# Graph attention, last stage: the low parts are made from a copy of the high parts in PSUM

## The chip, the cores and the metric

The kernel runs on one core of a Trainium2 chip. The metric is the device time of one execution in microseconds (us). Given for the kernel before are the times of three executions, and one more execution that the hardware profiler recorded.

The engines go by their names in the profile: PE (TensorE, matrix products; PEld is its weight load), DVE (VectorE), ACT (ScalarE), POOL (GpSimd, which here also issues the indirect DMAs that gather rows) and SP (SyncE, which issues the other DMAs).

## The reference

Two layers of a relational graph attention network over 3125 nodes of 768 numbers and 53125 edges that are sorted by their target node; then the input is added and each row is normalised. For each layer:

```python
xr = jnp.einsum('nd,rdf->rnf', x, W)          # three relations
oi = xr[etype, dst]
oj = xr[etype, src]
alpha = jax.nn.leaky_relu(oi @ q + oj @ k, 0.2)
m = jax.ops.segment_max(alpha, dst, num_segments=n_nodes)
e = jnp.exp(alpha - m[dst])
z = jax.ops.segment_sum(e, dst, num_segments=n_nodes)
a = e / (z[dst] + EPS)
msg = (a[:, :, None] * oj.reshape(-1, heads, out_ch)).reshape(-1, heads * out_ch)
out = jax.ops.segment_sum(msg, dst, num_segments=n_nodes) + b
```

The first layer has four heads of 192, the second one head of 768. Between them stands an elu; at the end `_layernorm(x + out)`. Everything is float32.

## The kernel before

The kernel has four parts in a row: the sorting data of the edges and the attention weights (`prepare`, `weights_kq`, `nodes_kq`), the first layer's rows and attention (`phase1`), the first layer's sums over edges together with the second layer's rows (`phase2`), and the last stage, `phase3`: the second layer's attention, its sums over edges, the residual and the normalisation. A second kernel stands behind an `If` for edge lists that do not fit the layout; it does not run with these inputs. The change is in `phase3` alone.

**Tiling.** The targets are cut into 25 blocks of 128 nodes (NB). A block's edges are cut into slots of 128 edges: 18 slots for each block (SL), 9 for the last, 441 slots in all (NK). For a slot, POOL gathers 128 rows of 772 float32 numbers from the table `tab2` in HBM with one indirect DMA (`gather`, which calls `gather_rows`, line L451). A row holds the 768 features, the key's part of the attention score, a 1 for the sum of the weights, and padding. The rows land in `gs`, six tiles of six slots each, so 36 slots are held.

**Sums.** For each slot the kernel multiplies a 128x128 selection matrix (which edge goes to which node of the block) by the slot's 128x772 rows, weighted by `p`, the exponential of the attention score. The product is added up in PSUM over the slots of a block (`acc`, two banks, two buffers). There are two ways for it, and `whole(k)` says which one a slot takes:

- A whole slot is one product in float32. DVE makes `selp`, the selection with the weights in it (L1062), and PE multiplies it by the gathered rows G (L1091, the rows `acc<-G,selp`; four records each slot).
- A split slot is two products in the float32r type. ACT makes the high part `H = p * G`, rounded to float32r (L1066); DVE, or POOL for the last 18 slots, makes the selection `sel` of ones and zeros (L1071 or L1069); DVE makes the low part `L = p * G - H` (L1080, function `low`); PE multiplies `sel` by H and by L (L1091, rows `acc<-H,sel` and `acc<-L,sel`).

With `WHOLE = (13, 25)`, 13 of each 25 slots are whole; of the last 18 slots (`late`) each third is.

`selp` and `sel` compare a row of the numbers 0 to 127 with each edge's node. The row lies in SBUF as `row` (frow in the profile); `phase3` copies it into a PSUM bank of its own, `rowp` (L959), for VectorE.

**Attention of a block.** DVE spreads the edges' node numbers from a PSUM product `bc` into `sT` (L980 on PE, L986 on DVE, five times each block); PE looks up the query's part with it (`pq`, L1000), DVE reduces it (L1006, L1008), `a_alpha` adds the key's part out of the gathered rows (L1015, which needs the block's last gather) and makes the leaky relu (L1017); PE turns the scores (L1022), DVE finds each node's largest with two scans (L1028, L1030), ACT takes the exponential (`e`, L1037), PE turns it back (L1041), DVE copies it to `p` (L1046).

**End of a block.** `e_y` divides and adds the residual on DVE (L1102), `e_n` makes the statistics (L1109 to L1113), `e_sd` takes a square root on ACT (L1117), `e_low` follows on DVE (L1122, L1124), `e_out` scales on ACT (L1130) and SP stores the rows. ACT changes its function table twice a block, once for the exponential and once for the root.

**Order.** All engines run instructions in the order of one Python loop that is written out by hand, and wait for each other by semaphores. An iteration k does, in this order: the gather of slot k; the sums of slot k - LAG (LAG = 29); the events of k, which are the attention and end steps, set by `when(...)`; and then

```python
            if 0 <= k - LAG + 2 < NK:
                low(k - LAG + 2)
            if 0 <= k - LAG + 3 < NK:
                high(k - LAG + 3)
```

`high` makes `selp`, or H and `sel`. A block's steps come at fixed iterations: counted from the block's end e, alpha at e + 2, the turn at e + 3, the scans at e + 4, exp at e + 5, the turn back at e + 6 and `p` at e + 7. The block's end steps follow at e + 30 to e + 37.

**PSUM in this stage.** Eight banks: `acc` four, `bc`, `pq`, `pa` and `rowp` one each.

Of the kernel before, what the change touches and what calls it, by code (L numbers as in the profile page):

```python
# [8 lines left out]
F32 = mybir.dt.float32  # L9
F32R = mybir.dt.float32r  # L10
F16 = mybir.dt.float16
BF = mybir.dt.bfloat16
I32 = mybir.dt.int32
AF = mybir.ActivationFunctionType
ALU = mybir.AluOpType
# [5 lines left out]
P = 128  # L21
# [17 lines left out]
CAP = SL * P  # L39
# [5 lines left out]

PART = 6

WHOLE = (13, 25)


@with_exitstack
def kernel(
# [32 lines left out]
    RW = D + 4  # L85
    HW = RW // 2
    CW = F1 + 1
    LL = FRONT + E + BACK
    NK = (NB - 1) * SL + SLL
    V, S, G, T = nc.vector, nc.scalar, nc.gpsimd, nc.tensor  # L90
# [16 lines left out]
    row = keep.tile([P, P], F32, name="frow")  # L107
# [10 lines left out]
    dl = keep.tile([P, NB, SL], F32, name="fdl")  # L118
# [146 lines left out]
    def split_parts(work, pts, w, name="t"):  # L265

        parts = []
        for i, pt in enumerate(pts):
            H, L = (work.tile([P, 2, w if name != "t" else 2 * P], F32R, name=f"{name}{s}{i}",
                              bufs=2 if name == "t" else 1) for s in "HL")  # L270
            S.copy(H[:, :, :w], pt[:, :, :w])
            V.tensor_sub(L[:, :, :w], pt[:, :, :w], H[:, :, :w].bitcast(F32))
            parts.append((H, L))
        return parts
# [179 lines left out]
    def start(b, into):  # L454
        if b not in into:
            into[b] = nc.sync.value_load(starts[0:1, b:b + 1], min_val=0, max_val=E)
        return into[b]

    def at(t, rw, off, ap, s):

        c = t[rw:rw + 1, bass.ds(s + (FRONT + off), 1)]
        return bass.AP(tensor=c.tensor, offset=c.offset, ap=ap)
# [282 lines left out]
    def phase2(work, psum, wH, wL):  # L745
# [25 lines left out]
        def whole(k):  # L771

            return k < 8 and k % 2 == 1

        def high(k):
            b, j = slot(k)
            g = gs[k % NG]
            if whole(k):
                sel = work.tile([P, H1, P], F32, name="L", bufs=3)
                for h in range(H1):  # L780
# [12 lines left out]
        def low(k):  # L793
# [4 lines left out]
            H = st[k][1]  # L798
            L = work.tile([P, RW], F32R, name="L", bufs=3)
            for h in range(H1):  # L800
                c = slice(h * CW, (h + 1) * CW)
                V.scalar_tensor_tensor(L[:, c], g[:, c], pall[:, b, j, h:h + 1], H[:, c].bitcast(F32),  # L802
                                       op0=ALU.mult, op1=ALU.subtract)
# [139 lines left out]
    def phase3(work, psum):  # L943
# [8 lines left out]
            V.memset(t, 0.0)  # L952
        blk = {}
        st = {}
        one = work.tile([1, P], BF, name="one", bufs=1)
        V.memset(one, 1.0)

        rowp = psum.tile([P, 512], F32, name="rowp", bufs=1)[:, :P]
        V.tensor_copy(rowp, row)  # L959

        def gather(k):
            b, j = divmod(k, SL)
            gather_rows(gs[k // PART % NT][:, k % PART, :], tab2, b, j)

        def a_load(b):
            s = blk[b] = {}
            r0 = start(b, regs)
            s["f"] = work.tile([SL, 3 * P + 1], F32, name="f", bufs=2)
            nc.sync.dma_start(s["f"], at(ed_d, 3, -P - 1, [[P, SL], [1, 3 * P + 1]], r0))
            s["d"] = work.tile([1, CAP], BF, name="d", bufs=2)  # L970
            nc.sync.dma_start(s["d"], at(dr_d, 0, 0, [[CAP, 1], [1, CAP]], r0))

        def a_spread(b, i):
# [21 lines left out]
        def a_q2(b):  # L995
            s = blk[b]
            nq = R * 3
            pq = s["pq"] = psum.tile([P, 512], F32, name="pq", bufs=1)
            for j in range(SL):
                T.matmul(pq[:, j * nq:(j + 1) * nq], s["sT"][:, j * P:(j + 1) * P],  # L1000
                         q2s[:, b].rearrange("p r s -> p (r s)"), start=True, stop=True)
# [46 lines left out]
        def whole(k):  # L1048

            return k % 3 == 0 if late(k) else k * WHOLE[0] % WHOLE[1] < WHOLE[0]  # L1050

        def late(k):

            return k >= NK - SL

        def high(k):
            b, j = divmod(k, SL)
            g = gs[k // PART % NT][:, k % PART, :]
            p = blk[b]["p"][:, j:j + 1]
            if whole(k):  # L1060
                sel = work.tile([P, P], F32, name="selp", bufs=4)
                V.tensor_scalar(sel, rowp, dl[:, b, j:j + 1], p, op0=ALU.is_equal, op1=ALU.mult)  # L1062
                st[k] = [sel, g]
                return
            H = work.tile([P, RW], F32R, name="H", bufs=4)
            S.activation(H, g, AF.Copy, scale=p)  # L1066
            sel = work.tile([P, P], F32R, name="sel", bufs=4)
            if late(k):
                G.tensor_scalar(sel, row, dl[:, b, j:j + 1], None, op0=ALU.is_equal)  # L1069
            else:  # L1070
                V.tensor_scalar(sel, rowp, dl[:, b, j:j + 1], None, op0=ALU.is_equal)  # L1071
            st[k] = [sel, H]

        def low(k):
            if whole(k):
                return
            b, j = divmod(k, SL)
            g = gs[k // PART % NT][:, k % PART, :]
            L = work.tile([P, RW], F32R, name="L", bufs=3)
            V.scalar_tensor_tensor(L, g, blk[b]["p"][:, j:j + 1], st[k][1].bitcast(F32), op0=ALU.mult, op1=ALU.subtract)  # L1080
            st[k].append(L)

        def sums(k):
            b, j = divmod(k, SL)
            sel, *parts = st.pop(k)
            if j == 0:
                blk[b]["acc"] = psum.tile([P, 2, 512], F32, name="acc", bufs=2)
            acc = blk[b]["acc"]
            for i, a in enumerate(parts):
                for c in range(2):  # L1090
                    T.matmul(acc[:, c, :HW], sel, a[:, c * HW:(c + 1) * HW], start=(j == 0 and i == 0),  # L1091
                             stop=(k in ends and i == len(parts) - 1))
# [45 lines left out]
        LAG = SL + 11  # L1138
        for b in range(NB):
            when(max(b * SL - 12, 0), a_load, b)  # L1140
            for i in range(5):
                when(max(b * SL - 4, 2) + 2 * i, a_spread, b, i)
                when(max(b * SL - 4, 2) + 1 + 2 * i, a_spread2, b, i)
            for d, f in ((10, a_q), (11, a_q2), (12, a_q3)):
                when(max(b * SL - 4, 2) + d, f, b)
            e = min((b + 1) * SL, NK)
            for d, f in ((2, a_alpha), (3, a_turn), (4, a_scan), (5, a_exp), (6, a_back), (7, a_put)):
                when(e + d, f, b)
            if b + len(xbs) < NB:
                when(e + LAG + 20, x_load3, b + len(xbs))  # L1150
            for d, f in ((1, e_y), (2, e_n), (5, e_sd), (6, e_low), (8, e_out)):
                when(e + LAG + d, f, b)
        for k in range(max(ev) + 1):
            if k < NK:
                gather(k)
            if 0 <= k - LAG < NK:
                sums(k - LAG)
            for f, a in ev.get(k, []):
                f(*a)
            if 0 <= k - LAG + 2 < NK:  # L1160
                low(k - LAG + 2)
            if 0 <= k - LAG + 3 < NK:
                high(k - LAG + 3)

    with tc.manual_schedule():
        with tc.tile_pool(name="share", bufs=1) as pool:
# [4 lines left out]
            with tc.tile_pool(name="wbuf", bufs=1) as wbuf:  # L1171
                wH = wbuf.tile([P, R * DT, D + 2], F32R, name="wH")
                wL = wbuf.tile([P, R * DT, D + 2], F32R, name="wL")
                with tc.tile_pool(name="pre", bufs=1) as pre:
                    qq = pre.tile([P, NB, H1, R], F32, name="qq")
                    with tc.tile_pool(name="work0", bufs=1) as work, tc.tile_pool(
                        name="psum0", bufs=1, space=PSUM
# [21 lines left out]
                    with tc.tile_pool(name="work1", bufs=1) as work, tc.tile_pool(  # L1199
                        name="psum1", bufs=1, space=PSUM  # L1200
# [4 lines left out]
            with tc.tile_pool(name="work3", bufs=1) as work, tc.tile_pool(name="psum3", bufs=1, space=PSUM) as psum:  # L1205
                phase3(work, psum)
# [538 lines left out]
```

## Time and profile before

| | |
|---|---|
| three executions, median (lowest to highest) | 2476.31 us (2463.49 to 2496.46) |
| the profiled execution's own time | 2296.29 us |
| its span, first to last instruction | 2294.5 us |
| mean granted clock of PE in it | 0.955 |
| PE, PEld busy | 2047.2 us (89%), 1758.8 us (77%) |
| DVE busy | 1685.4 us (73%) |
| ACT busy | 1172.9 us (51%) |
| POOL busy | 1749.5 us (76%) |
| HBM read, written | 428.40 MB, 94.04 MB |
| PE, DVE, ACT, POOL busy in 1610 to 2247 us, of 637.00 | 548.84, 523.56, 262.61, 502.22 us |

Shares of busy time are means over stages that differ; what sets the time of a stage is read from a window of the trace that holds this stage alone. A line of a group gives the line of the kernel, the engine, the operation, the names of what it writes and reads, the shapes and the count; behind the bar the busy time in us and the mean duration in ns; behind the second bar how long the engine was idle just before these instructions, and what ended most of that ("issue" is idle time for which the profile shows no reason). A line of waits gives who waited for whom, the sum in us, how often, and the longest. A line of the timeline gives the start and the duration in us, and in brackets the idle time before it. Matmuls overlap in the records, so a busy PE is not a PE at its peak.

### The profile page before, as it was taken

What the parts mean: (1) busy time and instruction counts of PE and PEld (TensorE: products, weight loads), DVE (VectorE), ACT (ScalarE), POOL (GpSimd) and SP (SyncE); (2) the same over time, 40 slices, a digit from 0 to 9 for tenths busy, and PEclk for the clock granted to TensorE, in tenths of its full rate; (3) what the DMA queues carried; (4) which work ended last, traced back from release to release, by engine and by line L of the source; (5) the groups of instructions that cost most, each with busy time, mean ns of one, the idle gap of its engine ahead of it and who ended that gap; (6) DMA issues with size and microseconds to landing.
All of it is one profiled execution on the core that took longest, in us unless ns stands there. A gap on an engine that the chain in (4) does not pass through costs nothing.

```text
span 2294.5 us, 37251 instructions
## 1 busy us (share of the span) xinstructions
PE 2047.2 (89%) x11055; PEld 1758.8 (77%) x11055; DVE 1685.4 (73%) x4377; ACT 1172.9 (51%) x2620; POOL 1749.5 (76%) x1685
## 2 busy tenths in 40 slices
PE   6998878998885899999999999999498898899886
PEld 5888878888885889999999999999255555555554
DVE  7734434434432899999999999995388888898887
ACT  5411111111111788888888888884144444444443
POOL 4267777777776888888888888883777777777773
PEclk9999999999998899999999999999699999999998
DMA  6554544444455977778777777775888888888882
GB/s 178 179 154 158 177 137 158 165 153 143 158 191 166 316 237 232 228 231 244 236 229 234 230 234 238 232 231 202 282 280 293 288 296 279 286 278 283 282 269 72
DMA packets 153593, 508.20 MB, mean 221 GB/s; under 512 B 40404, under 2 KB 53723, under 8 KB 153383
## 3 DMA queue, kind: packets, MB, share of 16 engines
q0 software_dynamic: 85472, 334.19, 48.1%
q1 hardware_dynamic: 57681, 155.56, 18.8%
q10 hardware_dynamic: 10230, 15.98, 2.2%
q8 instruction: 91, 1.49, 0.3%
q14 instruction: 119, 0.97, 0.1%
HBM read 428.40 MB, written 94.04 MB: 228 GB/s over the span
## 4 chain that ended last, share of the span: by engine, by line
PE 35%; DVE 14%; POOL 7%; issue 6%; DMA 5%; ACT 1%; POOLq 0%; DVEq 0%; ACTq 0%
PE po L876 15%; PE acc L821 11%; PE acc L1091 7%; DMA G<-ftab,ridx 4%; DVE L L1080 4%; POOL share L451 3%; POOL sel L790 2%; DVE selp L1062 1%; DVE L L802 1%; DVE sT L986 1%; POOL G L451 1%; DVE sel L1071 1%; DMA G<-ftab,rfirst 1%; PE pt L851 1%; DVE stats L1109 1%
## 5 line engine op out<-in xcount | busy, mean ns | idle before, releaser
L788 ACT ACTIVATE H<-share,pall 128x193 fp32r<-128x193 f32 x1748 | 644.0, 447 | 106.9 <-DMA share<-ftab,ridx 43.5
L802 DVE SCALAR_TENSOR_TENSOR L<-share,pall,H 128x193 fp32r<-128x193 f32 x1748 | 648.9, 437 | 28.6 <-ACT H L788 14.1
L876 PE MATMUL po<-wH,hT 128*128 128x386 f32 (+1 forms) x1800 | 533.2, 339 | 0.0
L451 POOL DMA_INDIRECT G<-ftab,ridx x378 | 432.5, 1144 | 115.2 <-issue 54.0
L451 POOL DMA_INDIRECT kt<-kt,ridx x378 | 405.7, 1073 | 115.2 <-issue 114.6
L451 POOL DMA_INDIRECT share<-ftab,ridx x378 | 428.6, 1134 | 81.4 <-DVE L L802 42.6
L629 PE MATMUL po<-wH,xT 128*128 128x384 f32 x1584 | 445.2, 354 | 0.4 <-issue 0.2
L1091 PE MATMUL acc<-G,selp 128*128 128x386 f32 x904 | 355.5, 519 | 1.1 <-DVE selp L1062 1.1
L876 PEld LDWEIGHTS po<-wH,hT 128*128 128x128 f32 x1800 | 334.6, 189 | 0.6 <-DVE hT L864 0.5
L876 PE MATMUL po<-wL,hT 128*128 128x386 f32 (+1 forms) x900 | 304.9, 339 | 0.0
L629 PEld LDWEIGHTS po<-wH,xT 128*128 128x128 f32 x1584 | 302.1, 196 | 2.9 <-DVE xT L616 0.5
L629 PE MATMUL po<-wL,xT 128*128 128x384 f32 x792 | 275.4, 348 | 0.0
L821 PE MATMUL acc<-H,sel 128*128 128x386 f32 x874 | 241.9, 358 | 22.0 <-POOL sel L790 12.1
L641 ACT COPY share<-po 128x384 f32<-128x384 f32 x144 | 69.0, 479 | 339.4 <-PE po L629 274.4
L1091 PEld LDWEIGHTS acc<-G,selp 128*128 128x128 f32 x904 | 169.7, 199 | 89.1 <-issue 23.0
L790 POOL TENSOR_SCALAR sel<-frow,fdl 128x128 fp32r<-128x128 f32 x291 | 224.8, 773 | 13.4 <-PE acc L821 1.5
L821 PE MATMUL acc<-L,sel 128*128 128x386 f32 x874 | 226.5, 340 | 0.0
L1080 DVE SCALAR_TENSOR_TENSOR L<-G,p,H 128x772 fp32r<-128x772 f32 x215 | 217.5, 1013 | 1.4 <-issue 0.7
L1066 ACT ACTIVATE H<-G,p 128x772 fp32r<-128x772 f32 x215 | 189.8, 927 | 47.5 <-issue 34.0
L821 PEld LDWEIGHTS acc<-H,sel 128*128 128x128 f32 x874 | 149.8, 189 | 55.7 <-POOL sel L790 46.7
L565 DVE TENSOR_TENSOR a<-qe,kt 128x72 f32<-128x72 f32 x25 | 5.9, 238 | 242.3 <-DMA kt<-kt,ridx 205.3
L876 PEld LDWEIGHTS po<-wL,hT 128*128 128x128 f32 x900 | 169.7, 189 | 0.0
(229 smaller groups left out, 2902.8 us busy)
## 6 DMA issues: line engine op xcount, KB each, us to landing
ftab<-r SPq DMA_DIRECT2D x75, 386.0 KB
ftab<-share SPq DMA_DIRECT2D x72, 386.0 KB
sT<-dr_d SPq DMA_DIRECT2D x25, 576.0 KB
share<-in_L_gnn_W_dram SPq DMA_DIRECT2D x36, 384.0 KB
w_d<-w2hl SPq DMA_DIRECT2D x18, 768.0 KB
share<-in_x_dram SPq DMA_DIRECT2D x25, 384.0 KB
xb_d<-share SPq DMA_DIRECT2D x25, 384.0 KB
xr<-in_x_dram SPq DMA_DIRECT2D x23, 384.0 KB
```

The lines of the kernel that those rows point to most:

```text
L451: G.indirect_dma_start(out=to, out_offset=None, in_=tab, in_offset=_index(i[:, j:j + 1]), bounds_check=NP * R - 1, oob_is_err=False)
L629: T.matmul(po[:, :HALF], xT[:, s, t, :], w[:, i, sl], start=(n == 0), stop=(n == 3 * DT - 1))
L641: S.copy(to, po[:, :HALF].rearrange("p (h f) -> p h f", h=2))
L788: S.activation(H[:, c], g[:, c], AF.Copy, scale=pall[:, b, j, h:h + 1])
L790: (V if k % 3 == 0 else G).tensor_scalar(sel, row, dl[:, b, j:j + 1], None, op0=ALU.is_equal)
L802: V.scalar_tensor_tensor(L[:, c], g[:, c], pall[:, b, j, h:h + 1], H[:, c].bitcast(F32), op0=ALU.mult, op1=ALU.subtract)
L821: T.matmul(acc[:, c, :HW], sel, a[:, c * HW:(c + 1) * HW], start=(j == 0 and i == 0), stop=(k in ends2 and i == 1), skip_group_check=True)
L851: T.transpose(pt[:, t // 3, (t % 3) * P:(t % 3 + 1) * P], s["ey"][:, t * P:(t + 1) * P], ident)
L876: T.matmul(po[:, :wd], hT[:, k, t, :], w[:, r * DT + t, sl], start=(t == 0 and n == 0), stop=(t == DT - 1 and n == 2))
L1066: S.activation(H, g, AF.Copy, scale=p)
L1080: V.scalar_tensor_tensor(L, g, blk[b]["p"][:, j:j + 1], st[k][1].bitcast(F32), op0=ALU.mult, op1=ALU.subtract)
L1091: T.matmul(acc[:, c, :HW], sel, a[:, c * HW:(c + 1) * HW], start=(j == 0 and i == 0), stop=(k in ends and i == len(parts) - 1))
```

## The change

- `rowp` goes. `sel` and `selp` read `row` in SBUF.
- In `high`, ACT copies H, once it is made, into a tile `Hp` in PSUM: two banks, one buffer, half of the columns in each. These are 14 of each 25 slots now, as `WHOLE` becomes `(11, 25)`; the last 18 slots keep their share.
- In `low`, DVE subtracts `Hp` in place of H; the two operands are taken as two halves of 386 columns.
- `low` and `high` of a slot come one iteration earlier (k - LAG + 3 and k - LAG + 4), with five buffers in place of four for `selp` and `sel` and four in place of three for L; H keeps four.
- `pq` takes its turn in the bank of `bc`, so that eight banks are enough: `acc` four, `Hp` two, `bc` with `pq`, `pa`.
- `d`, the edges' node numbers that `bc` is made of, has one buffer in place of two.

```diff
-WHOLE = (13, 25)
+WHOLE = (11, 25)
...
+        high_p = {}
         one = work.tile([1, P], BF, name="one", bufs=1)
         V.memset(one, 1.0)
-
-        rowp = psum.tile([P, 512], F32, name="rowp", bufs=1)[:, :P]
-        V.tensor_copy(rowp, row)
...
-            s["d"] = work.tile([1, CAP], BF, name="d", bufs=2)
+            s["d"] = work.tile([1, CAP], BF, name="d", bufs=1)
...
-            pq = s["pq"] = psum.tile([P, 512], F32, name="pq", bufs=1)
+            pq = s["pq"] = psum.tile([P, 512], F32, name="bc", bufs=1)
...
-                sel = work.tile([P, P], F32, name="selp", bufs=4)
-                V.tensor_scalar(sel, rowp, dl[:, b, j:j + 1], p, op0=ALU.is_equal, op1=ALU.mult)
+                sel = work.tile([P, P], F32, name="selp", bufs=5)
+                V.tensor_scalar(sel, row, dl[:, b, j:j + 1], p, op0=ALU.is_equal, op1=ALU.mult)
...
             S.activation(H, g, AF.Copy, scale=p)
-            sel = work.tile([P, P], F32R, name="sel", bufs=4)
-            if late(k):
-                G.tensor_scalar(sel, row, dl[:, b, j:j + 1], None, op0=ALU.is_equal)
-            else:
-                V.tensor_scalar(sel, rowp, dl[:, b, j:j + 1], None, op0=ALU.is_equal)
+
+            high_p[k] = psum.tile([P, 2, 512], F32, name="Hp", bufs=1)[:, :, :HW]
+            S.copy(high_p[k], H.bitcast(F32).rearrange("p (c f) -> p c f", c=2))
+            sel = work.tile([P, P], F32R, name="sel", bufs=5)
+            (G if late(k) else V).tensor_scalar(sel, row, dl[:, b, j:j + 1], None, op0=ALU.is_equal)
...
-            L = work.tile([P, RW], F32R, name="L", bufs=3)
-            V.scalar_tensor_tensor(L, g, blk[b]["p"][:, j:j + 1], st[k][1].bitcast(F32), op0=ALU.mult, op1=ALU.subtract)
+            L = work.tile([P, RW], F32R, name="L", bufs=4)
+            V.scalar_tensor_tensor(L.rearrange("p (c f) -> p c f", c=2), g.rearrange("p (c f) -> p c f", c=2),
+                                   blk[b]["p"][:, j:j + 1], high_p.pop(k), op0=ALU.mult, op1=ALU.subtract)
...
-            if 0 <= k - LAG + 2 < NK:
-                low(k - LAG + 2)
             if 0 <= k - LAG + 3 < NK:
-                high(k - LAG + 3)
+                low(k - LAG + 3)
+            if 0 <= k - LAG + 4 < NK:
+                high(k - LAG + 4)
```

## The prediction

> **What bounds the kernel now.** I read the page first: the span is 2294.5 us, and no engine is the bound of all of it. Then I cut the span by the view of windows, since the change touches the last stage alone, which runs from the first gather of tab2 at 1610 us to the end. Its steady part:
>
> ```profile
> 1685.00:2233.00 548.00, 493.65 (x2094) 302.22 (x2093) 471.92 (x1089) 241.83 (x288) 432.71 (x379) 0.96 0.86 284
> 2247.00:2294.50 47.50, 29.11 (x119) 20.52 (x117) 31.28 (x67) 16.68 (x22) 12.21 (x12) 0.89 0.10 34
> ```
>
> The columns are PE, PEld, DVE, ACT and POOL busy, the clock, the DMA share, GB/s. Everything but ACT looks full, so the groups of this stretch come next:
>
> ```profile
> L451 POOL DMA_INDIRECT G<-ftab,ridx x378 | 432.5, 1144 | 115.2 <-issue 54.0 <-PE acc L1091 15.3 <-DMA G<-ftab,ridx 12.5
> L1080 DVE SCALAR_TENSOR_TENSOR L<-G,p,H 128x772 fp32r<-128x772 f32 x182 | 184.3, 1012 | 0.0
> L1066 ACT ACTIVATE H<-G,p 128x772 fp32r<-128x772 f32 x182 | 160.7, 927 | 35.8 <-issue 30.8 <-PE acc L1091 3.9 <-ACT H L1066 0.7
> L1062 DVE TENSOR_SCALAR selp<-rowp,fdl,p 128x128 f32<-128x128 f32 x197 | 78.6, 401 | 0.0
> L1071 DVE TENSOR_SCALAR sel<-rowp,fdl 128x128 fp32r<-128x128 f32 x182 | 61.7, 339 | 0.0
> L1037 ACT ACT_TABLE_LOAD x22 | 28.2, 1283 | 0.4
> ```
>
> 378 gathers are 21 blocks of 18 slots, so a block takes 548 / 21 = 26.1 us. POOL is busy or in its fixed gap all of that: 432.5 + 115.2 = 547.7 us, 1.449 us a gather, and the gaps are 115.2 / 378 = 0.305 us each, whoever is named as releaser. POOL is the bound. The waits of the same stretch agree: VectorE runs into a wait for rows.
>
> ```profile
> DVE a L1015 <- DMA G<-ftab,ridx: 58.4, 17, 5.6
> ACT e L1037 <- DVE e L1033: 153.0, 21, 10.4
> ACT sd L1117 <- DVE sd L1113: 62.1, 21, 3.9
> ```
>
> With 4.5 us more that this wait has under "issue", VectorE stands 62.9 / 21 = 3.0 us a block, so it needs 23.1 itself. ACT's waits are for VectorE: it runs ahead and has time.
>
> Why does a gather take 1144 ns? The timeline of POOL, and below it VectorE's:
>
> ```profile
> 1870.00 1.01 POOL L451 DMA_INDIRECT G<-ftab,ridx  x1 [0.30 <-PE bc L980]
> 1871.32 1.01 POOL L451 DMA_INDIRECT G<-ftab,ridx  x1 [0.30 <-issue]
> ...
> 1901.43 1.65 POOL L451 DMA_INDIRECT G<-ftab,ridx  x1 [0.30 <-DVE sT L986]
> 1903.39 1.53 POOL L451 DMA_INDIRECT G<-ftab,ridx  x1 [0.30 <-PE pq L1000]
> 1905.22 1.79 POOL L451 DMA_INDIRECT G<-ftab,ridx  x1 [0.30 <-DVE sel L1071]
> ```
>
> ```profile
> 1901.19 1.00 DVE L1080 SCALAR_TENSOR_TENSOR L<-G,p,H 128x772 fp32r<-128x772 f32 x1
> ...
> 1903.03 1.00 DVE L1080 SCALAR_TENSOR_TENSOR L<-G,p,H 128x772 fp32r<-128x772 f32 x1
> ...
> 1905.11 1.01 DVE L1080 SCALAR_TENSOR_TENSOR L<-G,p,H 128x772 fp32r<-128x772 f32 x1
> 1906.05 0.40 DVE L1062 TENSOR_SCALAR selp<-rowp,fdl,p 128x128 f32<-128x128 f32 x1
> 1906.37 0.34 DVE L1071 TENSOR_SCALAR sel<-rowp,fdl 128x128 fp32r<-128x128 f32 x1
> 1906.63 1.01 DVE L1080 SCALAR_TENSOR_TENSOR L<-G,p,H 128x772 fp32r<-128x772 f32 x1
> ```
>
> While VectorE waits (1868.6 to 1872.5) a gather takes 1.01. One that starts inside an L ends 0.88 after that L: 1902.19 + 0.88 = 1903.07 against 1903.08, 1904.03 + 0.88 = 1904.91 against 1904.92, 1906.12 + 0.88 = 1907.00 against 1907.01. So L holds the gather up. An L that starts within a gather does not: the L of 1906.63, inside the last gather, takes its usual 1.01. The same lines give the cost from start to start on VectorE: L 0.94, selp 0.32, sel 0.26.
>
> [...] the stage before selects from the SBUF row,
>
> ```profile
> L790 DVE TENSOR_SCALAR sel<-frow,fdl x146: 270/276/730, 738.2 to 1571.4; 128x128 fp32r<-128x128 f32 x146
> ```
>
> at 276 ns (median) against 339 from rowp. [...]
>
> **The change part by part.** *Gathers.* L now reads G in SBUF and Hp in PSUM[...]: a gather falls toward 1.01 + 0.305 = 1.315 us. Left are the scan B, oh, a and al (two SBUF inputs, under 1.7 us a block) and the selections[...]. Between nothing and 0.06 a gather: I take 0.03. POOL then needs 1.345 × 18 = 24.2 us a block. DMA must move 284 × 26.1 / 24.2 = 306 GB/s, at a share of about 0.93; the trace has the room, not much more.
>
> *Mix.* In 18 slots 13/25 makes 9.36 whole and 8.64 split, 11/25 makes 7.92 and 10.08. PE: a pair of both starts every 2.01 us (timeline, 1905.26 and 1907.27), split-split-whole every 2.72 in the tail, so split is 0.71 and whole 1.30; PE saves 1.44 × 0.59 = 0.85 us a block, and gets nothing for it, as it is not the bound (18.3 us a block of slots, some 2.5 of small products).
>
> *VectorE's work.* Before 8.64 × (0.94 + 0.26) + 9.36 × 0.32 = 13.4 us. The selections fall by 63 ns at best and 30 if gathers hold them; I take 50: 10.08 × (0.94 + 0.21) + 7.92 × 0.27 = 13.7, so 0.35 more. L with one input in PSUM isn't seen at this size, but L1102 reads acc from PSUM and 768 columns in 1018 ns: nothing, at worst 0.1 each.
>
> *The copy on ACT.* 10.08 a block of 128x772. No row has SBUF to PSUM. The nearest, 128x768 from PSUM (L858), is 0.79; [...]y's ACTIVATE (L1130) 1.03 bounds it above. I take 0.79. ACT then needs 10.08 × (0.92 + 0.03 + 0.79) + two table loads 2.6 + y, e, sd 1.3 = 21.4 us of work: below POOL, but no longer idle.
>
> *The wait that is added.* Hp has one buffer (two banks), so a copy waits for the L before it, and the next L for the copy; behind the copy stand all of ACT's exp, sqrt and y, behind L all of VectorE. The loop is L 1.02 + 0.03 + copy 0.79 + 0.03 = 1.87 us from L to L. Against it VectorE's own pace, with the events of 18 iterations from its timeline: none in 0, 9, 10, 11, 14, 16, 0.1 to 1.9 us in the others. Two split slots in a row (2.16 a block) take 1.13 + events; the loop is 0.74 longer without events, 0.37 on average: 0.80. Split-whole-split (7.92 a block) takes 1.41 + two iterations' events; short in three places only: 0.46. The sqrt's table load and sd put 1.41 between a copy and the next H: H + copy then come 3.2 us after the last copy where VectorE's pace is 2.3: 0.65 after slack. The first slot of a block is now begun in the very iteration that makes p: H 0.92 and copy 0.79 lie between p and its L, where one iteration lay before: 0.35. exp and y: 0.3. Together 2.55; some fall on the same L, and 0.2 of waits for pq is there already. I take 1.8, with 0.9 and 3.2 as ends.
>
> *At nothing.* d with one buffer: SP's next load of it waits for PE's fifth spread, two iterations back, and is used eight later; x_load and stores behind it on SP have more room. pq in bc's bank: bc's last reader is two iterations earlier. sel and L one buffer more, H still four: fits. rowp's copy goes; the first gather waited for tab2, not for it. Gathers themselves are not moved.
>
> *Sum.* VectorE with the loop: 23.1 + 0.35 + 1.8 = 25.25 us a block, above POOL's 24.2, so it is the bound: 0.85 less than 26.1. Of 441 gathers the first 36 meet no L; 405 / 18 = 22.5 blocks: -19 us. The tail holds six split-split-whole: 2 × 1.87 = 3.74 against 2.72, +6, of which the earlier begin and the events there take 2: +4. Sum -15 us: 2296.3 (span 2294.5 and 1.8 around it) becomes 2281. The runs shown have a median 180 us above it; the profile doesn't say in which stage, and I carry -15 over: 2461.
>
> **Rivals.** *POOL decides* (0.27): the loop hides under events and gather waits, 24.2 a block, -43 + 4 = -39: 2437; at the floor of 1.315 and no tail cost -54: 2422. For it: ACT has idle time today, VectorE a 3 us cushion. Against: one buffer. *The Hp loop decides above 26.1* (0.19), the side of slower: copy 1.03 and L 0.1 longer make the loop 2.21; the same sum gives 4.05 of stalls, 2.9 after the same cut, and 1.0 for L: 23.1 + 0.35 + 1.0 + 2.9 = 27.35, +28 and 7 in the tail: 2511. It decides once stalls and longer L pass 2.65 us a block. *It does not do what it says* (0.06): [...]rows come no faster as DMA is full: period 26, 2476.
>
> **How the numbers follow.** Forecast 0.48 (-5 to -30: 2446 to 2471). The range takes in the POOL floor, wider by the scatter of the runs (2463 to 2496): 2412, and most of the slower case: 2508. About 2% is what a measurement of this kernel can tell from no change; that is 50 us. Only POOL at its floor passes it, with some of the case where slower runs weigh this stage more: 0.18; of the slower case half: 0.09; the rest 0.73.
>
> **What would show it.** Gathers near 1.04 us mean; if still over 1.12, the lock step is wrong. Gaps on POOL over 0.31: another bound; if none, POOL decides. L about 1.02, the copy 0.75 to 0.85, waits of L for the copy and of the copy for L some 2 us a block each. The wait of a for G small. If a still waits 2 us a block, the stalls were overrated; if a block exceeds 26.1 us, underrated.

## The result and the profile after

The change does not bring the 15 us: it costs about 27. The median is 2506.93 us against 2479.69 before, the ratio 1.011 [1.0074, 1.0147]. The forecast was 2461; the number lies inside the range, on the other side of no change.

The executions fell on chips of two speeds: before takes 2293 to 2295 us on two of them and 2480 to 2519 on the others, and the profile that the prediction reads (span 2294.5) is of the first kind, the result and the profile of after (span 2504.8, own time 2506.62) of the second. Each chip was used for one set of runs only, so the chip and the hour are not told apart; "kind of chip" below means the kind of run. The experiments are set against before on their own chip; this section alone sets after's profile beside one of the other kind. The us in the tables are medians of all executions, while the ratios compare the fast executions of both kernels, so the two need not agree to the last per mille.

The windows of after: the steady part (from one block's first gather to another's, 21 blocks apart), and the end from the last gather on. Columns as before: PE, PEld, DVE, ACT and POOL busy, clock, DMA share, GB/s.

```profile
1852.00:2429.60 577.60, 490.91 (x2076) 307.24 (x2075) 485.53 (x1118) 438.64 (x530) 385.06 (x379) 0.93 0.82 270
2441.40:2504.80 63.40, 38.30 (x167) 26.72 (x165) 40.03 (x85) 39.91 (x50) 8.28 (x13) 0.87 0.10 34
```

Over 21 blocks ACT went from 242 to 439 us busy, POOL from 433 to 385, and the DMAs moved 270 GB/s where the profile before had 284. No engine is full: PE is busy for 85% of the 577.6 us, DVE for 84%. The groups of the steady part:

```profile
L451 POOL DMA_INDIRECT G<-ftab,ridx x378 | 384.9, 1018 | 192.3 <-PE acc L1090 76.9 <-issue 73.3 <-PE bc L978 10.0
L1078 DVE SCALAR_TENSOR_TENSOR L<-G,p,Hp 128x772 fp32r<-128x772 f32 x212 | 214.6, 1012 | 45.3 <-issue 20.3 <-ACT Hp L1067 19.9 <-ACT H L1064 3.5
L1064 ACT ACTIVATE H<-G,p 128x772 fp32r<-128x772 f32 x213 | 198.5, 932 | 15.8 <-DVE selp L1060 5.7 <-issue 4.4 <-DVE p L1044 2.9
L1067 ACT COPY Hp<-H 128x772 f32<-128x772 f32 x212 | 171.1, 807 | 112.9 <-DVE L L1078 77.7 <-issue 25.9 <-ACT H L1064 7.2
L1069 DVE TENSOR_SCALAR sel<-frow,fdl 128x128 fp32r<-128x128 f32 x211 | 64.2, 304 | 0.0
L1060 DVE TENSOR_SCALAR selp<-frow,fdl,p 128x128 f32<-128x128 f32 x167 | 60.2, 361 | 0.0
```

The first line holds both halves of the story. A gather takes 1018 ns, not 1144, and the 135 gathers of the stage that begin inside an L take 1013: L no longer holds them up (the "lock step" of the prediction). But POOL is idle for 192.3 us where its fixed gaps are 378 × 0.305 = 115.3, and the 77 us beyond them come for the most part behind `PE acc`: a gather waits for a buffer that PE has not yet read out. Before, the sums waited for rows; now rows wait for the sums. The waits of the same stretch say who holds the sums:

```profile
DVE L L1078 <- issue: 20.3, 38, 1.2
DVE L L1078 <- ACT Hp L1067: 19.9, 36, 1.1
DVE oh L1004 <- PE acc L1090: 17.8, 15, 2.7
ACT Hp L1067 <- DVE L L1078: 77.7, 93, 3.5
```

L waits for the copy, and the copy for the L before it (on this kind of chip VectorE waits for PE besides, at `oh`). The wait of `a` for G, 58.4 us before, is not in the list at all.

### The profile page after: what moved, and what is told of

It reads as the page before. It is cut to its first block, busy times and chain, and to the rows that moved or that the text cites. A ratio compares the mean times of both kernels' runs of the same rounds, so it can differ in the third digit from the quotient of the medians.

```text
span 2504.8 us, 37700 instructions
## 1 busy us (share of the span) xinstructions
PE 2102.0 (84%) x11055; PEld 1791.0 (72%) x11055; DVE 1701.6 (68%) x4410; ACT 1402.8 (56%) x2903; POOL 1681.8 (67%) x1685
## 3 DMA queue, kind: packets, MB, share of 16 engines
q14 instruction: 124, 1.02, 0.1%
## 4 chain that ended last, share of the span: by engine, by line
PE 27%; DVE 13%; issue 7%; POOL 7%; ACT 6%; DMA 5%; another core or an unknown queue 3%; DVEq 0%; POOLq 0%; ACTq 0%
PE po L876 9%; PE acc L1090 7%; PE acc L821 7%; DVE L L1078 4%; POOL share L451 4%; DMA share<-ftab,ridx 3%; ACT H L788 3%; DVE L L802 3%; POOL sel L790 2%; PE po L629 1%; ACT Hp L1067 1%; POOL G L451 1%; ACT H L1064 1%; DVE selp L1060 1%
## 5 line engine op out<-in xcount | busy, mean ns | idle before, releaser
L802 DVE SCALAR_TENSOR_TENSOR L<-share,pall,H 128x193 fp32r<-128x193 f32 x1748 | 647.8, 436 | 26.8 <-ACT H L788 17.2
L629 PE MATMUL po<-wH,xT 128*128 128x384 f32 x1584 | 475.4, 370 | 108.6 <-issue 70.9
L451 POOL DMA_INDIRECT G<-ftab,ridx x378 | 384.9, 1018 | 192.3 <-PE acc L1090 76.9
L629 PEld LDWEIGHTS po<-wH,xT 128*128 128x128 f32 x1584 | 318.8, 207 | 135.2 <-issue 89.8
L1090 PE MATMUL acc<-G,selp 128*128 128x386 f32 x768 | 310.7, 529 | 0.2 <-issue 0.2
L629 PE MATMUL po<-wL,xT 128*128 128x384 f32 x792 | 287.7, 363 | 16.5 <-issue 16.5
L1078 DVE SCALAR_TENSOR_TENSOR L<-G,p,Hp 128x772 fp32r<-128x772 f32 x249 | 252.1, 1013 | 58.7 <-ACT Hp L1067 32.6
L1067 ACT COPY Hp<-H 128x772 f32<-128x772 f32 x249 | 200.9, 807 | 144.0 <-DVE L L1078 106.7
L821 PE MATMUL acc<-H,sel 128*128 128x386 f32 x874 | 241.6, 357 | 19.2 <-POOL sel L790 8.7
L1064 ACT ACTIVATE H<-G,p 128x772 fp32r<-128x772 f32 x249 | 232.1, 932 | 16.4 <-DVE selp L1060 5.7
L1090 PEld LDWEIGHTS acc<-G,selp 128*128 128x128 f32 x768 | 146.4, 202 | 84.7 <-issue 22.3
L1090 PE MATMUL acc<-H,sel 128*128 128x386 f32 x498 | 182.6, 449 | 15.9 <-DVE sel L1069 15.9
```

The costliest lines, as they stand in the source:

```text
L451: G.indirect_dma_start(out=to, out_offset=None, in_=tab, in_offset=_index(i[:, j:j + 1]), bounds_check=NP * R - 1, oob_is_err=False)
L629: T.matmul(po[:, :HALF], xT[:, s, t, :], w[:, i, sl], start=(n == 0), stop=(n == 3 * DT - 1))
L1067: S.copy(high_p[k], H.bitcast(F32).rearrange("p (c f) -> p c f", c=2))
L1078: V.scalar_tensor_tensor(L.rearrange("p (c f) -> p c f", c=2), g.rearrange("p (c f) -> p c f", c=2), blk[b]["p"][:, j:j + 1], high_p.pop(k ...
```

## Experiments

Gathers that run ahead of the sums make the stage look shorter up to the last gather and longer behind it, so I cut it by L instead, of which each split slot has one: from the first gather to the first L of the last 18 slots (**body**, 423 slots), the twelve L of these slots (**late**), and **rest**. All starts are from the timelines (0.94 us after the first where one line merges two L). The last three columns are of one profile each: two profiles of before, on the first kind of chip, differ by 2.3 us in the body and 1.6 in late.

| kernel | us, ratio to before on its chip | body | late | rest |
|---|---|---|---|---|
| before (the profile of the prediction) | 2296.29 | 650.6 | 16.6 | 17.2 |
| e0, before once more | 2298.78 | 652.9 | 18.2 | 17.2 |
| e7, after | 2300.84, 1.0032 [1.002, 1.0043] | 651.0 | 23.0 | 17.0 |
| e1, no copy | 2296.22, 1.0007 [0.9996, 1.0017] | 654.3 | 18.3 | 17.8 |
| e5, no copy, L from PSUM | 2239.06, 0.9745 [0.9718, 0.9773] | 598.5 | 17.2 | 17.7 |
| e6, as e5, with ACT's work | 2245.63, 0.9776 [0.9747, 0.9804] | 599.6 | 17.7 | 19.8 |
| e2, after with 13 of 25 | 2249.4, 0.9798 [0.9753, 0.9842] | 600.1 | 23.0 | 17.1 |
| f1, before on a slower chip | 2510.86 | 690.9 | 16.6 | 17.3 |
| f2, after on that chip | 2530.66 | 701.3 | 23.0 | 17.0 |

**Before and after once more on the first kind of chip** (e0, e7: no edit).

> The kernel before, profiled once more, since its first profile (2294.5 us) lies 180 us under its median and the profile of the changed kernel (2504.8 us) does not. Theory (the loop through Hp in the last stage): the last stage takes again about 684 us from its first gather to the end, and the other 150 to 200 us of the two profiles' difference lie before it, in stages that the change does not touch. Rival (the last stage itself varies that much): it takes 720 us or more here.

> The changed kernel once more, on the chip on which the kernel before takes 2295 us. Theory (the loop L, copy, L through the one Hp, and what stands behind it): a block of 27.0 to 27.4 us against 26.1 before and against 23.7 to 23.8 of the runs in which no L waits for a copy; last stage about 720 to 733 us against 684 to 688, the whole 2325 to 2345 us (ratio 1.013 to 1.022). Rival (most of the loss shown first was in earlier stages): last stage under 700, ratio under 1.007.

e0 took 2298.78 us. Its last stage is 688.4 us long (684.4 in the first profile), that of after's profile 733.0; its first gather comes at 1608.6 us and after's at 1771.8. So 163 of the 208 us between these two profiles lie ahead of the stage that the change touches. e7 took 2300.84 us where before took 2292.9: +8. I had expected 2325 to 2345; a last stage of 691.0 us and a ratio of 1.0032 are the rival's numbers, so on this kind of chip the loop takes back what the gathers gain, and little more. The profile of e7, a window of 21 blocks of gathers, its waits, and below them VectorE and ACT in the last 18 slots:

```profile
1684.90:2228.20 543.30, 474.61 (x2062) 300.48 (x2062) 477.13 (x1101) 433.78 (x524) 384.44 (x378) 0.95 0.86 286
```

```profile
ACT Hp L1067 <- DVE L L1078: 83.5, 143, 2.9
POOL G L451 <- PE acc L1090: 53.1, 59, 5.4
DVE L L1078 <- ACT Hp L1067: 52.5, 84, 1.2
```

```profile
2271.28 1.02 DVE L1078 SCALAR_TENSOR_TENSOR L<-G,p,Hp 128x772 fp32r<-128x772 f32 x1 [0.93 <-ACT Hp L1067]
2272.22 0.36 DVE L1060 TENSOR_SCALAR selp<-frow,fdl,p 128x128 f32<-128x128 f32 x1
2273.23 1.02 DVE L1078 SCALAR_TENSOR_TENSOR L<-G,p,Hp 128x772 fp32r<-128x772 f32 x1 [0.65 <-ACT Hp L1067]
2275.18 1.02 DVE L1078 SCALAR_TENSOR_TENSOR L<-G,p,Hp 128x772 fp32r<-128x772 f32 x1 [0.93 <-ACT Hp L1067]
```

```profile
2272.39 0.81 ACT L1067 COPY Hp<-H 128x772 f32<-128x772 f32 x1 [0.27 <-DVE L L1078]
2274.34 0.81 ACT L1067 COPY Hp<-H 128x772 f32<-128x772 f32 x1 [0.27 <-DVE L L1078]
```

This is the loop, bare: L ends 2272.30, copy 2272.39 to 2273.20, L 2273.23 to 2274.25, copy 2274.34, L 2275.18. From L to L it is 1.95 us, whether a `selp` lies between or not: VectorE waits for ACT, ACT for VectorE, each of them some of the time. The 210 L of the window are 210 / 10.08 = 20.8 blocks, so VectorE waits 52.5 / 20.8 = 2.5 us a block for the copy.

**Is L's second operand in SBUF the cause of the long gathers, and the loop the price?** e1 takes the copy away and has L read H in SBUF again; e5 takes the copy and the loop away and leaves L an operand in PSUM (zeros, so that it leaves out the subtraction of the high parts); e6 does so too and has ACT do work like the copy's, with no L waiting for it.

```diff
# e1
-            high_p[k] = psum.tile([P, 2, 512], F32, name="Hp", bufs=1)[:, :, :HW]
-            S.copy(high_p[k], H.bitcast(F32).rearrange("p (c f) -> p c f", c=2))
...
-                                   blk[b]["p"][:, j:j + 1], high_p.pop(k), op0=ALU.mult, op1=ALU.subtract)
+                                   blk[b]["p"][:, j:j + 1], st[k][1].bitcast(F32).rearrange("p (c f) -> p c f", c=2), op0=ALU.mult, op1=ALU.subtract)
# e5: the copy goes as in e1; L subtracts a PSUM tile that is set to zero once
+        hps = psum.tile([P, 2, 512], F32, name="Hp", bufs=1)[:, :, :HW]
+        V.memset(hps, 0.0)
...
+                                   blk[b]["p"][:, j:j + 1], hps, op0=ALU.mult, op1=ALU.subtract)
# e6: as e5, and in the place of the copy
+            S.copy(H, H.bitcast(F32))
```

> The changed kernel without the copy: L reads H in SBUF again, all else of the change stays (11 of 25, one iteration sooner, row in SBUF). Theory (the loop L, copy, L costs VectorE, and PE behind it, some 4 us a block): VectorE's waits before L go to nothing, gathers are held up again, by 10.08 instead of 8.64 L a block: 1.01 + 0.137 x 10.08 / 8.64 + 0.305 = 1.475 us a gather, POOL decides at 26.6 us a block against 27.2 with the copy: last stage 700 to 710 us against 733. Rival (the mix of 11 makes VectorE or PE late): 27 us or more stay.

> The changed kernel with L reading a tile in PSUM that is filled once with zeros; there is no copy, so the high parts are not subtracted. What is left is the change without its price. Theory: gathers stay at 1.02 us, VectorE has no wait before L, and the block falls to VectorE's own need or POOL's, 23.5 to 24.5 us: last stage 650 to 665 us, the whole 60 to 80 us under the changed kernel. Rival (DMA or PE sets the block[...]): 26 us or more.

> As the one before, but ACT copies each H onto itself in SBUF: ACT has the work of the copies (about 0.83 us each), and no L waits for it, since L reads the tile of zeros. Theory (it is the wait through one buffer, not ACT's work): within 0.7 us a block of the run without any copy, some 24.5 us. Rival (ACT's 22 us of work a block, with two table loads, is itself the bound, or makes exp late): 26.5 to 27.5 us a block.

The gathers of the steady part in e1, then in e5:

```profile
L451 POOL DMA_INDIRECT G<-ftab,ridx x378 | 436.2, 1154 | 115.2 <-issue 52.4 <-DMA G<-ftab,ridx 14.9 <-PE acc L1088 11.3
```

```profile
L451 POOL DMA_INDIRECT G<-ftab,ridx x378 | 385.6, 1020 | 115.2 <-issue 43.6 <-DMA G<-ftab,ridx 12.5 <-PE acc L1089 11.0
```

Same number of L, same selections from SBUF; the difference is where L's second operand lies, and that L no longer waits for H (1.9 us of waits in all of e1's window): 1154 ns against 1020. Sorted by what VectorE does when they start, the gathers that begin inside an L took 1434 ns on average in e1 (127 of them), 1353 in before (157) and 1013 in e5 (154); with VectorE idle it is 1009 to 1010 in all three. In both windows POOL is never idle beyond its gaps (115.2), so POOL decides in both; e1 is at (436.2 + 115.2) / 21 = 26.3 us a block (26.6 expected), e5 at (385.6 + 115.2) / 21 = 23.85, and 0.9745. So it is shown that an L with both operands in SBUF holds gathers up and one with an operand in PSUM does not (1434 against 1013 ns), and so is the room behind it: 2.9% (1.0032 - 0.9745), some 66 us, lie between e5 and after, and these two differ in the copy and in what L waits for. e6 came to 2245.63 us, 0.9776 [0.9747, 0.9804], with casts of 836 ns in place of copies of 807. ACT's work then costs at most 6.6 us of the difference (of the 7.1 between the two profiles 3.4 lie ahead of the stage), the waiting the rest, some 59. Both stand at POOL's floor, so a gain beyond that floor would not show here.

**Is it the exponential, late behind copies on ACT?** e4 asks for it an iteration sooner.

```diff
-            for d, f in ((2, a_alpha), (3, a_turn), (4, a_scan), (5, a_exp), (6, a_back), (7, a_put)):
+            for d, f in ((2, a_alpha), (3, a_turn), (4, a_scan), (4, a_exp), (6, a_back), (7, a_put)):
```

> The changed kernel with one event moved: exp is issued an iteration sooner, right behind the scans, so that it stands on ACT ahead of the H and the copy of that iteration. Theory (exp with its table load is stuck behind a copy that waits for L, PE's turn back waits for exp, and VectorE then for PE's pq and bc): VectorE's waits for PE, 1.5 us a block, go to a third, a block of 25.8 to 26.2 us, 22 to 30 us less than the changed kernel. Rival (only the direct waits of L for the copy count): under 8 us less.

2316.75 us, 1.0087 [1.0057, 1.0117], so 16 us worse than e7 where 22 to 30 better were expected. PE's wait for e fell from 12.1 to 4.7 us, and L's for the copy rose from 52.5 to 61.3. The late exponential is not what costs the time; put ahead of an H and its copy, it made L wait longer.

**Does a finer hand-over help?** e9 makes copy and L in two halves, each with its own bank.

```diff
+            high_p[k] = [psum.tile([P, 512], F32, name=f"Hp{c}", bufs=1)[:, :HW] for c in range(2)]
+            for c in range(2):
+                S.copy(high_p[k][c], H.bitcast(F32)[:, c * HW:(c + 1) * HW])
...
+            for c, hp in enumerate(high_p.pop(k)):
+                V.scalar_tensor_tensor(L[:, c * HW:(c + 1) * HW], g[:, c * HW:(c + 1) * HW],
+                                       blk[b]["p"][:, j:j + 1], hp, op0=ALU.mult, op1=ALU.subtract)
```

> The changed kernel with the copy and L each in two halves, and Hp as two tiles of one bank: the same columns, 0.1 us more a slot on each of the two engines, but the first half of the next copy may start when the first half of L is done. Theory (one buffer makes the loop): L to L falls from 1.87 us to some 1.25, below VectorE's own pace, waits before L fall under 0.5 us a block, VectorE gets 1.3 us more work: a block of 24.3 to 25.5 us, last stage 650 to 675 us, faster than before by 10 to 35 us. Rival (ACT's order, table loads and exp, not the buffer): a block stays at 26.5 or more.

2286.87 us, 0.9964 [0.9944, 0.9983], 14 better than e7. The wait is nearly gone,

```profile
DVE L L1080 <- ACT Hp L1068: 17.5, 35, 0.9
```

but a half L takes 607 ns and a half copy 482, so two halves cost 0.20 and 0.16 us more than a whole: work replaced most of the waiting, and VectorE is busy for 496 of 529 us. I had expected 10 to 35 us less than before; it is 6.

**Is it the mix?** With 11 of 25, split slots follow each other directly in 3 places of 25; with 13 of 25 never, and there are 12 split slots in 25 in place of 14.

```diff
-WHOLE = (11, 25)
+WHOLE = (13, 25)
```

> The changed kernel with 13 of 25 slots whole, as before. No two split slots stand in a row then. Theory: the waits that two in a row make (0.8 us a block by the prediction's working) and 1.44 copies a block go, PE gets 0.85 us more, which hides: a block of 25.7 to 26.3 us, 20 to 35 us less than the changed kernel, no slower than before. Rival (PE sets the block in the changed kernel, as VectorE waits for it): 13 is slower than 11.

2249.4 us, 0.9798. The same loop, the same copy, and its steady part

```profile
1675.50:2176.30 500.80, 475.19 (x2078) 295.49 (x2076) 451.13 (x1083) 385.75 (x467) 385.67 (x378) 0.99 0.90 310
```

is POOL's 23.85 us a block again, with the DMAs at 310 GB/s. L still waits,

```profile
DVE L L1078 <- ACT Hp L1067: 31.6, 57, 1.2
```

but 31.6 / 21 = 1.5 us a block fit into what VectorE has left (500.80 - 451.13 = 49.7 us idle in all). The mix alone is worth 51 us, more than the 20 to 35 that were expected. Two things change with it, and this run does not part them: from e7 to e2 VectorE's work falls from 22.9 to 21.5 us a block, as there are 1.44 L and their selections less, and its wait for the copy from 2.5 to 1.5. Where the waits lie can be seen by giving the L of the timeline to the split slots in order. In e7, 18.2 us fall on slots whose predecessor is split too; the other 34 fall on the first, third and fourth slot of a block (20.2, from the making of `p` on), on the tenth and eleventh (10.3, behind the root's table load) and on the last (4.0, behind the exponential's). In e2 the first part is gone and the rest is still 31.6. The mix does nothing for the last 18 slots, whose share it does not touch: late is 23.0 here too.

**On the slower chips.** e10, f3 and f5 are one kernel: 13 of 25, and the last 18 slots take L from H in SBUF without a copy (there are no rows left to gather then). e11 and f4 are the same with 11, e13 and f6 with 15; e12 has `low` and `high` in their old iterations; f1 is before and f2 after.

```diff
# e10, f3, f5 (e11, f4: 11; e13, f6: 15)
+WHOLE = (13, 25)
...
+            high_p[k] = H.bitcast(F32).rearrange("p (c f) -> p c f", c=2)
+            if not late(k):
+                high_p[k] = psum.tile([P, 2, 512], F32, name="Hp", bufs=1)[:, :, :HW]
+                S.copy(high_p[k], H.bitcast(F32).rearrange("p (c f) -> p c f", c=2))
# e12
-                low(k - LAG + 3)
+                low(k - LAG + 2)
...
-                high(k - LAG + 4)
+                high(k - LAG + 3)
```

> 13 of 25 whole with the copy (2249 us), and the last 18 slots without it. Theory: POOL's gathers keep the steady block at 23.85 us, the tail falls from 57 to about 50 us: 2241 to 2244 us, ratio 0.977 to 0.979. Rival (the tail is bound elsewhere at 13 of 25): 2249.

> The changed kernel, but for the last 18 slots L reads H in SBUF, with no copy[...]. Theory (the tail of three slots split, split, whole is paced by the loop, 3.9 us against 2.72, and that is 13 us of the 64 after the last gather): the tail falls to 50 to 53 us, the whole by 10 to 14 us, to 2287 to 2291 us, just under the kernel before. Rival (the tail is late for another reason, such as POOL's selections): under 4 us less.

> The changed kernel with low and high where they were before, not an iteration sooner. Prediction's own term: p then stands an iteration ahead of the first slot of a block, 0.35 us a block or 8 us go. Rival (L's iteration of lead over PE is worth more than that: PE then waits for L and holds gathers' buffers longer): no change or up to 15 us slower.

> As the one before with 15 of 25 whole: fewer copies and fewer low parts still, 0.85 us more of PE a block. Theory (POOL's 1.01 + 0.305 and a little for the selections is the floor, both engines fit under it): the same as with 13 within 4 us, waits before L under 0.7 us a block. Rival (PE, or its clock, becomes the bound): 24.5 us a block or more, 10 to 20 us slower than with 13.

> The kernel before, for a profile on the same chip as the next three. If the chip is one on which it takes about 2290 us: last stage 684 to 690 us, a block 26.0 to 26.3. If it is one on which it takes about 2490 us, theory (the extra there comes from waits that any order of the last stage meets, [...]fetches that no engine explains): last stage 700 to 715 us, a block 26.6 to 27. Rival (before is immune, as POOL decides and VectorE has slack): 685 to 692 us there too.

> The changed kernel beside it. First kind of chip: last stage 691 us, a block 25.9 to 26.2, tail 64. Second kind: 730 to 735 us, a block 27.4, VectorE waits 1 us a block for PE's pq besides the waits for the copy.

> 13 of 25 with the copy, the last 18 slots without it. First kind of chip: POOL decides, 23.85 us a block, tail 50 us, 2241 to 2244 us, ratio 0.977 to 0.979. Second kind: ratio 0.99 to 1.003, blocks near 27 us.

> The changed kernel without copies for the last 18 slots. First kind of chip: tail 50 to 53 us for 64, 2287 to 2291 us. Second kind: tail 58 us (as once measured there), ratio 1.004 to 1.007.

> 13 of 25 with the copy, the last 18 slots without it. Where the kernel before takes about 2293 us: POOL decides, 23.85 us a block, tail 50 to 54 us for 57, 2241 to 2246 us, ratio 0.977 to 0.980. Where it takes about 2510 us: 0.993 to 0.999 again, tail 54 us.

> 15 of 25 likewise. Theory (POOL's gathers are the floor where the chip lets them): the same time as with 13 within 4 us, waits before L under 0.7 us a block. Rival (PE is late with 10.8 whole slots a block): 10 us or more slower than with 13.

| kernel | us | ratio to before |
|---|---|---|
| before, on the chips of e10 to e13, of f1 to f4, of f5 and f6 | 2518.68; 2512.12; 2482.52 | |
| 13 of 25, late from SBUF (e10; f3; f5) | 2520.78; 2507.72; 2479.44 | 1.0012 [0.9982, 1.0042]; 0.9958 [0.9932, 0.9985]; 0.9942 [0.9912, 0.9972] |
| 11 of 25, late from SBUF (e11; f4) | 2532.74; 2522.62 | 1.0057 [1.0029, 1.0085]; 1.0062 [1.0025, 1.01] |
| 15 of 25, late from SBUF (e13; f6) | 2519.2; 2477.63 | 0.998 [0.9935, 1.0025]; 1.0041 [1.0001, 1.0081] |
| after, not sooner (e12) | 2549.59 | 1.0057 [1.0013, 1.0102] |

With the late copies gone, late falls to 17.3 us (e11), as without any copy. 13 of 25 stays ahead of 11, as on the first chips, but by half a per cent (the intervals overlap) and by one; 15 brings nothing more. The 2241 to 2246 us that were expected of e10, f3 and f5 were for the first kind of chip, on which none of them ran. e12 tells nothing: its interval covers what 11 of 25 costs here anyway, so whether the earlier iterations help stays open.

Why is so little left? The last stage takes 724.7 us in f1 and 741.2 in f2, 10 and 6 more than the most that was expected of this kind. f1, the profile of before on a slower chip, has POOL's idle at 146.6 us and not 115.2: POOL is not the only bound there, so a shorter gather should have less to give (argued; e5 was not run on such a chip). VectorE's waits in it, and then those of f2:

```profile
DVE oh L1006 <- remote: 30.9, 6, 9.5
DVE oh L1006 <- PE acc L1091: 13.3, 7, 3.6
```

```profile
DVE oh L1004 <- PE acc L1090: 24.0, 15, 4.4
DVE L L1078 <- ACT Hp L1067: 23.1, 42, 0.8
```

`oh` waits for `pq` from PE, up to 9.5 us at once, a wait that is small on the faster kind (2.9 us in all in the steady part of the prediction's profile, 0.2 in e7). With 13 of 25 (f3) VectorE still stands 68 us of 572 behind PE's sums, where e2 has none of it. PE's products themselves are not slower: inside a whole slot they start 325 ns apart (median) in before, e2, f1 and f3 alike (327 in after; a record lasts 487 ns, so they overlap). What makes PE late on these chips, no run settles: it comes under `remote` or behind PE's own sums.

## Why the prediction was wrong

**Right: the bound, and why.** On the first kind of chip POOL decided at 26.1 us a block, and L held the gathers up through VectorE's second operand in SBUF. Gathers were to fall to 1.04 us and fell to 1.018; e1 against e5 shows the cause by one operand: 1154 ns with two SBUF inputs, 1020 with one. No L of before has an operand in PSUM; that such an L would not hold a gather up was my estimate. I gave what else holds gathers up, scans and selections, 0.03 us a gather; it is 0.01 (1020 against 1009 undisturbed). Of the scans it is B, with two SBUF inputs: gathers that begin inside it took 1169 ns in before (17 of them) and 1140 in after (7), inside F, with one of two in PSUM, 1009 in both (13 and 15). DMA had the room: 310 GB/s at a share of 0.90, predicted 306 at 0.93.

**Right: the sizes of the new work.** The copy takes 807 ns (taken 0.79), L from PSUM 1006 to 1014 (nothing added), VectorE's need without waits 23.6 us a block: 477.13 / 20.8 = 22.9 busy, and 13.7 us of the window's idle time that is not the copy's, 0.66 a block (predicted 23.1 + 0.35).

**Right: the edits at nothing.** e1 has every edit but the copy and stands at 1.0007; e5 has them too and runs at POOL's floor. None of `d`, `pq` in `bc`'s bank, the buffers and the earlier iterations holds a block above 23.85 us. This is shown on the first kind of chip alone.

**Wrong: the cut from 2.55 to 1.8.** I summed the stalls place by place, got 2.55 us a block, and then took a third off because "some fall on the same L". Measured are 2.5. That the sum came so close is partly luck: two split slots in a row cost 0.87 (0.80 in the sum), but the start of a block 0.97, where the sum has 0.35 for the first slot and 0.46 for all alternating ones, and root and exponential less than I gave them. Why the stalls did not overlap can only be argued: in a loop, a late L makes the next copy late as well, so one stall is handed on and not absorbed. With 2.5 in the sum it reads 23.1 + 0.35 + 2.5 = 25.95, just below before's 26.1: the gain was mostly the discount. Counted by the sums (first L to first late L, 423 slots or 23.5 blocks) before takes (2260.72 - 1644.26) / 23.5 = 26.23 us a block and e7 (2264.76 - 1648.29) / 23.5 = 26.23. The term of -19 us is +0.4 (-1.9 against the profile of e0). It is the second rival's mechanism, the Hp loop, with the price not of a longer copy or L but of the full stalls.

**Nearly right: the end.** Twelve late L were to cost +6, with 2 off for the slots ahead of them: +4. They cost +6.4 on both kinds of chip (16.6 to 23.0; +4.8 against e0's 18.2), so about what the loop alone makes. The loop is 1.95 and not 1.87: the copy starts 0.09 us after L, where I took 0.03. The 13 to 15 us by which the stretch behind the last gather grows (49.1 to 63.8) are more than this because gathers now run further ahead: 21 L come behind the last gather in e7, 17 before.

**Sum on the first kind of chip:** +0.4 + 6.4 - 0.2 = +6.6 in the stage where I had -15, and +2.7 when e0 stands for before; measured +8 (2300.84 against 2292.9).

**Not seen: the other kind of chip.** I read -15 from a profile of 2294.5 us and carried it to runs 180 us longer, without asking whether POOL bounds those. f1 to f2 the body grows by 10.5 us, late by 6.4, the rest by -0.3, and the stages ahead by 3.2 (first gather at 1784.4 and 1787.6), together 19.8, one profile each. From first L to first late L the kernels with 11 of 25 and the copy take 27.3 to 27.75 us a block in four profiles on these chips (after, e11, f2, f4), before 27.2 in its one. The late part is explained; in the body, L's waits for the copy (23.1 us, and 15.5 under `issue`) are there, the rest lies in waits for PE whose cause is open. So of the 27 us of the result a part stays unexplained.

**The mix was booked as PE's affair and 0.35 us of VectorE.** In the prediction's own prices the old mix with the cheaper selections takes 8.64 × 1.15 + 9.36 × 0.27 = 12.5 us of VectorE, so the mix costs 13.7 - 12.5 = 1.2 a block; the 0.35 sets the gain of the selections against it. Measured are 1.4 us of work and 1.0 of waits more (e7 against e2), as it also makes split slots neighbours. e2 shows that the copy through PSUM with the old mix gains 2.0% where after loses 0.3%. That is the version that beats both on the first kind of chip; on the others its relative with the late slots from SBUF stands about half a per cent below before in two of three comparisons (0.2 and 0.1% by the medians in the table). e2 itself was not run there.

## What to carry to other kernels

When two engines hand one buffer to and fro, add up the loop (here 1.02 + 0.81 + two hand-overs = 1.95 us) and set it against the spacing of its users in the order that they really come: here 29 of 45 split slots behind another split one had to wait, and of the others only those at the start of a block and behind a table load, 56 of 164. When an edit has two parts, price each against the kernel without it: the gain of one hid the cost of the other in a net 0.35 us. Sum stalls in full, and give no discount that no line of the profile shows. Where a producer runs ahead, measure a stage at the consumer: the gathers of e7 came at 25.9 us a block while the sums stood at 26.2. And read whether the bound of the profile is also the bound of the runs whose time is forecast.

## What the runs showed of the hardware

- An ACT copy from SBUF to PSUM of 128x772 float32 took 807 ns (after, e7), of 128x386 482 (e9); the same copy within SBUF, to float32r, 836 (e6).
- An L with one operand in PSUM took what one with both in SBUF took (1006 to 1014 ns in e5, e7 and after, against 1012 in before and e1), and an L of half the columns 607 (e9).
- Selections of 128x128 from SBUF took 304 and 361 ns (after) where those from PSUM took 339 and 401 (before). Those of after that began inside a gather took longer than the others, `sel` 316 ns against 279 and `selp` 370 against 341; in before there was no such difference (339 against 340, 401 both). Those from SBUF do hold up a gather that begins inside one: 1065 (`sel`, 24 gathers) and 1050 ns (`selp`, 51) on average in e5, against 1008 (63) inside selections from PSUM in before. As few gathers begin so, the mean rose by 0.01 us only.
- The kernel before took 8 to 10% longer on some of the chips (2480 to 2519 us against 2293 to 2295), most of it ahead of the last stage (first gather at 1784.4 us in f1, 1610.1 in the profile of the prediction).
